# S1 T1 by quarters in the third and fourth pair of five more matrices of a relational graph layer

## The chip, the cores and the metric

The kernel runs on one core of one Trainium2 chip. The metric is device microseconds of one execution; the median over several runs is quoted, and the profile comes from one further execution.

## The reference

A graph layer over 1250 nodes with 1024 features, 20000 edges and 8 edge types:

```python
h = maximum(layernorm(x), 0)
u = h @ root + bias
for r in range(8):
    mask = edge_type == r
    sums = segment_sum(h[src] * mask[:, None], dst)       # by node
    cnt = segment_sum(mask, dst)
    u = u + (sums / maximum(cnt, 1)[:, None]) @ weight[r]
z = concatenate([u, h], axis=1) @ w_gate + b_gate
out = x + tanh(u) * z + h * (1 - z)
```

All in float32.

## The kernel before

**Matrices.** There are eleven products of the node features with a 1024 x 1024 matrix, in this order: eight `weight[r]` (s = 0 to 7), `root` (s = 8), the lower half of `w_gate` (s = 9), and the upper half (s = 10), which is applied to u. The text counts them one to eleven, so "matrix nine" is s = 8. The multiplication by `weight[r]` comes before the sum over edges: row blocks of h W_r go to `y` in DRAM, and rows of `y` are gathered edge by edge later.

**Pairs.** The 1250 nodes are ten blocks of 128 rows. Block i and block i + 5 form pair i; `product` handles one pair with one matrix, and `step(s, i)` calls it. Matrix s runs over pairs i = 0 to 4, the first to the fifth pair of the text. A pair is a 2 x 2 matrix of blocks (two blocks of rows by two halves of K), and `product` multiplies it with the 2 x 2 halves of the matrix in seven products instead of eight (Strassen's scheme in Winograd's form): A11 B11 (`p1`), A12 B21 (`p2`), S4 B22 (`p3`), A22 T4, S1 T1 (`p5`), S2 T2 and S3 T3 (`p7`), where S are sums of A blocks (`left`) and T of B blocks (`make_t1` to `make_t4`, L195 to L207). Each is four calls of a 128 x 128 by 128 x 512 matmul at L511.

**By quarters.** Two neighbouring pairs (first and second, third and fourth) together make some of the seven products once more in that scheme, on quarters: seven products, each two calls of 128 x 256 at L255, instead of eight calls of 128 x 512. Class `Second` does it for A12 B21 (`e` in `step`), `Third` for S4 B22 (`q`), `First` for A11 B11 (`first`), and `Fifth` for S1 T1 (`root`). Their own sums are made on VectorE in one shared buffer, `room`, four operations at a time: `sums` (L309 to L312) and `next_sums` (L315 to L318), the same two functions for `Third`, `First` and `Fifth`. So a class's `sums` can be made only when TensorE has read the ones before. `Fifth.begin`, `second`, `early` and `late` are the four places in the even pair's call where its matmuls stand; copies to and from its banks are L424, L432 and L439 on ScalarE, additions L434 and L445 on VectorE.

The function `fifths(s, i)` says in which matrices and pairs S1 T1 is made by quarters: in matrices two to five for all pairs, in six to ten for the first and second only.

**Banks.** PSUM has eight: `ps` four that rotate, `ps_b` two, `ps_n` and `ps_q` one each. `narrow[0]`, set from `fifths(s, i)`, sends the sums of S1 T1 and what is added to them into `sum_bank(0)`, which is `ps_n`, or `sum_bank(1)`, one of the four `ps` banks that is taken once and then held in `kept`. Where `narrow[0]` turns false, `kept` is cleared and the bank rotates again; the next time it is taken, `touch` (L134) writes it once with a matmul. The fourth pair's sum in `sum_bank(1)` is added to a row by L352 in `Third.last_to`; L351 and L353 beside it do so for `ps_n` and `ps_q`. In the fifth pair S1 T1 is made whole at L511, with `odd` 1.

**Order.** Each engine executes in the order in which the code issues. `product` calls `done()` at several places, the slots; each calls `between(j)`, which is `beside(j)` of `step` and, through it, the work of the edges: generators `edges` spread over the slots by `spread` (weights 10, 8, 13, 11, 8 for the five pairs). One step of it is `add_slot`: a gather of 128 rows of `y` by POOL (L1560) into one of five `got` buffers, and, some steps later, its addition to `u` on VectorE (L1565). It runs in matrices six to ten: one group of edges up to matrix eight, the second in nine and ten. `filled(name)` puts the matmuls by quarters of other classes between the seven products; the table of what goes where is `fill` in `step`. In a call with `Fifth` there is one slot more, `between(TICK)` in `p7`.

In the fourth pair's call, `fill["first"]` makes `e.seventh()` and, with `root`, `e.to_first(to)` (L282, L283), `q.first(...)`, `e.fourth()`, `e.to_second(t[0])` (L289, L290) and `e.fourth_to_second(t[0])` (L293): the matmuls that end A12 B21's quarters and the additions of them to the rows. `e.second()` later in that call takes a `ps` bank.

Of the kernel before, what the change touches and what calls it, by code (L numbers as in the profile page):

```python
# [21 lines left out]
def tile_rgcn_highway(  # L22
# [61 lines left out]
    TICK = 9  # L84
    LEFTS_AT = 6
    FIFTHS = (1, 4)
# [59 lines left out]
    def lead():  # L146

        return psum.tile([P, 512], F32, name="ps_b", bufs=2)
# [346 lines left out]
    def product(aop, w, to, between=lambda j: None, last=None, pieces=1, whole=True,  # L495
# [13 lines left out]
        def add(b, i, fresh=False, at=slice(0, Q), ks=range(KQ)):  # L509
            for k in ks:  # L510
                nc.tensor.matmul(b[:, at], aop[:, i, k, :], w.of[i][:, k, at],  # L511
                                 start=(fresh and k == 0), stop=(k == KQ - 1),
                                 skip_group_check=True)

        def done():
            between(step[0])
            step[0] += 1

        def filled(name):
            if fill and name in fill and fill[name]():  # L520
                done()
                return True
            return False
# [39 lines left out]
        def p1():  # L563
            if first is None:
                b = lead()
                add(b, A11, True)
            else:
                b = first.late() if head else first.to1
            if root and head:
                root.sums()  # L570
                first.fifth_to()
            nc.scalar.copy(c11, b)  # L572
            if root and head:
                root.second()
            done()
            filled("first")
            return b

        def p5(c=None):
# [14 lines left out]
        if root and head:  # L594
            root.begin()
            c = root.to0
            if inner:
                inner.c0 = c
            b = p1()
        elif first and head and early is None and "first" not in fill:  # L600
            c = inner.hold() if inner else sum_bank(odd) if narrow[0] else bank()
            add(c, S1, True, ks=range(KQ // 2))
            b = p1()
            p5(c)
        elif first and head:
            c = p5()
            b = p1()
        else:
            b = p1()
            if second:  # L610
                second()
                p2()
            c = p5()
# [74 lines left out]

    def fifths(s, i=0):

        return s >= FIFTHS[0] and (s <= FIFTHS[1] or i < 2)

    waiting, waiting_third, waiting_first, waiting_fifth = {}, {}, {}, {}
    at_call = [0, 0]
# [9 lines left out]
    def step(s, i, between=lambda j: None, second=None):  # L704

        two = paired(s, i)
        narrow[0] = fifths(s, i)
        if not narrow[0]:
            kept.clear()
# [6 lines left out]
        if two and i % 2 == 0:  # L716
            waiting[i] = Second(fac[s], i), t[0]
            if fifths(s, i):
                waiting_fifth[s, i] = Fifth(fac[s], i, room, p5_room)
# [13 lines left out]
        def beside(j):  # L733
# [28 lines left out]
            if (s, i, j) == (0, 0, 3) or (s > 0 and (i, j) == (3, int(thirds(s) or fifths(s)))):  # L762
                new.load_first()
# [205 lines left out]
    with ExitStack() as early:  # L969
# [20 lines left out]
        class Normed:  # L990
# [13 lines left out]
            def spread(self):  # L1004
                n = self.n
                nc.vector.bn_aggr(self.mv[:n], self.st[:n].rearrange("p a b -> p (a b)"))
                nc.scalar.activation(self.sd[:n], self.mv[:n, 1:2], AF.Sqrt, bias=eps[:n])
# [115 lines left out]
        first = ix1.tile([P, NCH], F32, name="first")  # L1123
# [391 lines left out]
        while going[0]:  # L1515
            s, i = next(steps)
# [11 lines left out]
    with ExitStack() as edges_part:  # L1528
# [89 lines left out]
        def spread(e, total, parts):  # L1618

            said = [0, 0]  # L1620
            parts *= 10

            def between(j):
                said[0] += (10, 8, 13, 11, 8)[at_call[0]]
                while said[1] < min(total, -(-total * said[0] // parts)):
                    next(e, None)
                    said[1] += 1
                if said[0] == parts:
                    for _ in e:
                        pass  # L1630

            return between
# [36 lines left out]
        def beside(e, total, s, i, last):  # L1669


            between = spread(e, total, 7 * ((last - s) * NP + NP - i))
            while s <= last:
                step(s, i, between)
                s, i = next(steps, (NM, 0))
            return s, i

        s, i = next(steps)
        while s <= EARLY:
            step(s, i)  # L1680
            s, i = next(steps)
# [21 lines left out]
        class Passes:  # L1703
# [45 lines left out]
            def next(self):  # L1749
                nc.vector.tensor_single_scalar(self.done, self.done, float(-MORE), op=OP.add)  # L1750
# [21 lines left out]
        while s < R0[1]:  # L1772
            step(s, i, on)
            s, i = next(steps)
# [14 lines left out]
        s, i = beside(first_group, sum(K[0]) + LATE + 1, s, i, R0[2] - 1)  # L1789
# [146 lines left out]
        while s < NM - 1:  # L1936
# [8 lines left out]
            s, i = next(steps, (NM, 0))  # L1945
# [86 lines left out]
```

## Time and profile before

| what | value |
|---|---|
| median of 3 runs | 1329.66 us (1327.80 to 1329.93) |
| profiled execution | 1325.06 us, its span 1323.3 us |
| granted TensorE clock | 0.998 |
| POOL L1560 gathers | 193, 1.32 us of POOL each |
| DVE L1565 edge additions | 193, 1.28 us each, 38.9 us idle before them |
| PE L511 into `ps_b` | 1464 matmuls, 658.3 us |

Busy times of the engines overlap each other, and those of pipelined matmuls overlap too, so costs of matmuls are taken from start to start. An engine's idle time matters only where another waits for it.

### The profile page before, as it was taken

How to read it: one execution, taken by the hardware profiler on the slowest of the kernel's cores; microseconds unless marked ns; L12 is line 12 of the kernel's file. 1: busy time of each engine (PE TensorE's matmuls, PEld its weight loads, DVE VectorE, ACT ScalarE, POOL GpSimd, SP SyncE). 2: the span in 40 equal slices, each digit the busy share in tenths (PEclk: the TensorE clock that was granted, in tenths of full speed). 3: DMA queues.
4: the chain of work that ended last, by engine and by line, in shares of the span. 5: the costliest groups of instructions: out<-in, count | busy, mean ns of one | idle time of the engine just before them, and what ended most of it. 6: DMA issues, size and time to landing. Idle time of an engine off the chain costs nothing.

```text
span 1323.3 us, 14353 instructions
## 1 busy us (share of the span) xinstructions
PE 1309.9 (99%) x4280; PEld 747.0 (56%) x4280; DVE 1032.2 (78%) x2171; ACT 277.9 (21%) x509; POOL 642.6 (49%) x981
## 2 busy tenths in 40 slices
PE   9999999999999999999999999999999999999997
PEld 5444565556455546655655655665565566544443
DVE  7768977797783776558977988897788889867974
ACT  3352121121112212211221211122122112122210
POOL 0001766666666675412453545456465546624732
PEclk9999999999999999999999999999999999999999
DMA  8976566753734253444748779788789957979961
GB/s 312 300 231 165 98 115 136 153 82 82 170 113 115 57 143 65 68 161 157 250 136 309 252 272 366 268 282 283 255 282 335 362 187 256 312 269 297 331 173 60
DMA packets 119397, 273.22 MB, mean 206 GB/s; under 512 B 33438, under 2 KB 45106, under 8 KB 119184
## 3 DMA queue, kind: packets, MB, share of 16 engines
q1 hardware_dynamic: 59120, 122.06, 31.7%
q0 software_dynamic: 44064, 118.20, 28.0%
q10 hardware_dynamic: 16128, 31.98, 7.9%
q8 instruction: 34, 0.56, 0.2%
q14 instruction: 51, 0.42, 0.1%
HBM read 210.73 MB, written 76.46 MB: 217 GB/s over the span
## 4 chain that ended last, share of the span: by engine, by line
PE 87%; DMA 4%; DVE 4%; issue 3%; POOL 1%; SPq 1%; ACT 1%; POOLq 0%; DVEq 0%
PE ps_b L511 42%; PE ps L255 19%; PE ps L511 10%; PE ps_n L511 4%; PE ps_b L255 4%; PE ps_n L255 3%; PE ps_q L255 2%; PE ps_q L511 2%; DMA xt<-in_x_dram 1%; DMA got<-hr_dram,node 1%; DMA w<-in_L_gnn_weight_dram 1%; DVE h_op L492 1%; DMA h_op<-in_L_gnn_b_gate_dram 0%; POOL out_dram L903 0%; SPq L983 0%
## 5 line engine op out<-in xcount | busy, mean ns | idle before, releaser
L511 PE MATMUL ps_b<-w,h_op 128*128 128x512 f32 x1464 | 658.3, 594 | 1.0 <-ACT row L615 0.8
L511 PEld LDWEIGHTS ps_b<-w,h_op 128*128 128x128 f32 x1464 | 275.2, 190 | 301.2 <-issue 292.7
L1560 POOL DMA_INDIRECT got<-y,idx x193 | 255.4, 1324 | 277.5 <-DVE u L1565 182.1
L1565 DVE SCALAR_TENSOR_TENSOR u<-got,w_of,u 128x1024 f32<-128x1024 f32 (+1 forms) x193 | 246.8, 1282 | 38.9 <-DMA got<-y,idx 36.3
L1209 POOL DMA_INDIRECT table<-row_col,at_i x157 | 183.3, 1168 | 119.4 <-issue 84.4
L511 PE MATMUL ps<-w,h_op 128*128 128x512 f32 (+1 forms) x392 | 174.1, 586 | 0.8 <-ACT row L589 0.8
L511 PEld LDWEIGHTS ps<-w,h_op 128*128 128x128 f32 x392 | 73.5, 190 | 84.0 <-issue 78.7
L255 PE MATMUL ps<-inner 128*128 128x256 f32 x420 | 106.1, 380 | 0.0
L255 PEld LDWEIGHTS ps<-inner 128*128 128x128 f32 x420 | 79.2, 190 | 20.7 <-issue 9.4
L255 PE MATMUL ps<-w,h_op 128*128 128x256 f32 x340 | 88.2, 382 | 1.0 <-ACT w L272 1.0
L255 PEld LDWEIGHTS ps<-w,h_op 128*128 128x128 f32 x340 | 63.7, 190 | 29.3 <-issue 20.7
L537 ACT COPY row<-ps_b 128x512 f32<-128x512 f32 x53 | 31.1, 586 | 225.4 <-PE ps_b L511 225.4
L615 ACT COPY row<-ps_b 128x512 f32<-128x512 f32 x54 | 31.7, 586 | 216.0 <-PE ps_b L511 216.0
L511 PE MATMUL ps_n<-w,h_op 128*128 128x512 f32 x168 | 75.6, 593 | 0.0
L255 PE MATMUL ps<-w,w 128*128 128x256 f32 x288 | 70.6, 380 | 0.0
L255 PEld LDWEIGHTS ps<-w,w 128*128 128x128 f32 x288 | 54.4, 190 | 17.2 <-issue 11.0
L1217 POOL MEMSET apart<- 128x1 f32 x471 | 54.6, 116 | 18.1
L659 ACT COPY row<-ps_b 128x512 f32<-128x512 f32 x40 | 23.4, 586 | 186.2 <-PE ps_b L511 165.1
L543 DVE TENSOR_TENSOR row<-row 128x512 f32<-128x512 f32 x44 | 30.2, 686 | 39.6 <-ACT row L537 39.6
L1326 DVE SCALAR_TENSOR_TENSOR junk<-k_bc,key_col,before 128x128 f32<-128x128 int16 x157 | 55.0, 350 | 4.2
L511 PEld LDWEIGHTS ps_n<-w,h_op 128*128 128x128 f32 x168 | 31.7, 190 | 37.7 <-issue 37.1
L572 ACT COPY row<-ps_b 128x512 f32<-128x512 f32 x54 | 31.8, 588 | 84.8 <-PE ps_b L511 80.5
(254 smaller groups left out, 1568.1 us busy)
## 6 DMA issues: line engine op xcount, KB each, us to landing
y<-row SPq DMA_DIRECT2D x72, 512.0 KB
w<-in_L_gnn_weight_dram ACTq DMA_DIRECT2D x21, 1024.0 KB
w<-in_L_gnn_weight_dram SPq DMA_DIRECT2D x10, 1024.0 KB
w<-lefts_dram SPq DMA_DIRECT2D x16, 512.0 KB
w<-in_L_gnn_w_gate_dram ACTq DMA_DIRECT2D x6, 1024.0 KB
k_bc<-keys_dram SPq DMA_DIRECT2D x39, 128.0 KB
l_bc<-los_dram SPq DMA_DIRECT2D x39, 128.0 KB
h_dram<-h_op SPq DMA_DIRECT2D x9, 512.0 KB
```

Of the source, the lines that this page charges most:

```text
L255: nc.tensor.matmul(p, a[:, k, :], b[:, k, :], start=(fresh and k == 0), stop=(k == 1), skip_group_check=True)
L511: nc.tensor.matmul(b[:, at], aop[:, i, k, :], w.of[i][:, k, at], start=(fresh and k == 0), stop=(k == KQ - 1), skip_group_check=True)
L537: nc.scalar.copy(d, b)
L543: nc.vector.tensor_add(c22, c if lone else c22, d)
L572: nc.scalar.copy(c11, b)
L615: nc.scalar.copy(c12, b)
L659: nc.scalar.copy(c21, b)
L1209: ins = nc.gpsimd.indirect_dma_start(out=table[:, :], out_offset=bass.IndirectOffsetOnAxis(ap=at_i[:n, c:c + 1], axis=0), in_=row_col[:n, ...
L1217: nc.gpsimd.memset(apart, 0.0)
L1326: nc.vector.scalar_tensor_tensor(junk, o["k_bc"][:, i, :], key_col[:, c:c + 1], before, op0=OP.is_equal, op1=OP.mult, accum_out=rank[:, c: ...
L1560: nc.gpsimd.indirect_dma_start(out=t[:n], out_offset=None, in_=y[g][:, :], in_offset=bass.IndirectOffsetOnAxis(ap=at[:n, d, k:k + 1], axis=0),
L1565: nc.vector.scalar_tensor_tensor(u[:n], t[:n], w, u[:n], op0=OP.mult, op1=OP.add)
```

## The change

`fifths` now holds for all matrices from the second on and all pairs, so S1 T1 of the third and fourth pair goes by quarters in matrices six to ten too. With it `narrow[0]` stays true in these matrices, and `kept` is not cleared in them. `fill` for the third pair is then the one for `root and q` (`e.first()` and `q.second` after S3 T3, `e.sixth()` at the end), and `e.seventh()` and `e.to_first(to)` move into the fourth pair's `fill["first"]`. In the odd pairs of matrices with both `Fifth` and `Third`, `filled("first")` now stands ahead of that slot's `done()`. `between` counts the slot `TICK` for the edges only in the first pair.

```diff
@@ product, p1
             if root and head:
                 root.second()
-            done()
-            filled("first")
+            if root and inner and not head:
+                filled("first")
+                done()
+            else:
+                done()
+                filled("first")
             return b
@@ 
     def fifths(s, i=0):
 
-        return s >= FIFTHS[0] and (s <= FIFTHS[1] or i < 2)
+        return s > 0
@@ spread
             def between(j):
-                said[0] += (10, 8, 13, 11, 8)[at_call[0]]
+                if j != TICK or at_call[0] == 0:
+                    said[0] += (10, 8, 13, 11, 8)[at_call[0]]
                 while said[1] < min(total, -(-total * said[0] // parts)):
                     next(e, None)
                     said[1] += 1
```

## The prediction

> **What bounds the kernel now.** I read the page's first and fourth parts, then windows over the stretches that the change touches, then the order of time on TensorE and VectorE around their ends. The page first (busy time by engine, and the shares of the chain that ended last):
>
> ```profile
> PE 1309.9 (99%) x4280; PEld 747.0 (56%) x4280; DVE 1032.2 (78%) x2171; ACT 277.9 (21%) x509; POOL 642.6 (49%) x981
> ...
> PE 87%; DMA 4%; DVE 4%; issue 3%; POOL 1%; SPq 1%; ACT 1%; POOLq 0%; DVEq 0%
> ```
>
> TensorE is the chain. Between 350 and 1170 us its matmuls stand end to end: the view of waits names one wait of PE there, of 0.5 us. So work taken from PE in matrices six to ten is time, unless PE begins to wait. The next view is windows over the third and fourth pair of one matrix: matrix five (which already makes S1 T1 of these pairs by quarters), then seven, nine and ten (which don't). Columns: length, busy time of PE, PEld, DVE, ACT, POOL, granted clock, DMA share, GB/s.
>
> ```profile
> 543.30:581.56 38.26, 38.26 (x139) 25.60 (x138) 20.36 (x52) 9.77 (x20) 14.13 (x15) 1.00 0.32 89
> ...
> 772.69:811.68 38.99, 38.99 (x125) 23.31 (x124) 31.18 (x37) 8.57 (x17) 23.52 (x21) 1.00 0.85 299
> ...
> 1002.99:1041.98 38.99, 38.99 (x126) 23.31 (x125) 30.93 (x38) 8.57 (x17) 26.25 (x21) 1.00 0.96 337
> 1118.15:1157.11 38.96, 38.96 (x126) 23.28 (x124) 31.31 (x41) 8.57 (x17) 24.83 (x19) 1.00 0.94 312
> ```
>
> Matrix five is the pattern for PE, but not for the rest: its DVE is busy 20.4 us of 38.3 and its DMA 0.32. In seven to ten DVE has 31 us of work in the same stretch, with the additions of gathered edges (L1565, 1.26 us each from start to start) in the same queue.
>
> **What PE saves.** Each f32 call of the code shows as two matmuls. S1 T1 of two pairs is now 16 matmuls of 512 columns, 3.435 us for each 8. By quarters it is seven products of 4 matmuls of 256 columns at 0.863 us. That is 6.87 against 6.04, a gain of 0.83. The pattern says the same with all that surrounds it: 38.26 less 0.11 for the two transposes of L1657 that only matrix five has is 38.15, against 38.99: 0.84 a matrix, 4.2 in five matrices. The bank that `sum_bank(1)` holds is no longer given up at the third pair, so the `touch` in matrices seven to ten goes: matrix six, which has none, takes 114.88 us from one fifth pair to the next (581.56 to 696.44) and matrix eight 115.13 (811.68 to 926.81). I take 0.25 each, 1.0 in four. Together 5.2 us off PE.
>
> The Trainium skill, "Perfetto Trace Analysis", section "Matmuls", holds larger matmuls to be more efficient where possible, which speaks against halving 512 columns; the rows above price the halves at no loss, so by the trace this part of the rule costs 0 here.
>
> **What it adds.** Per matrix DVE gets ten operations: `Fifth.sums` and `next_sums` (each 0.34 + 0.60 + 0.34 + 0.60 = 1.88, starts of the first pair's in matrix seven at 738.93 to 740.80), L434 and L445 (0.34 each): 4.4 us. ACT gets three copies (0.36, 0.37, 0.57: 1.3 us beside 8.6 of 39, free). DVE's idle in the stretch is 38.99 - 30.93 = 8.1 in matrix nine, 7.7 in ten, 7.8 in seven; afterwards some 2.6. POOL and SP keep their order; `TICK` not being counted in the third pair keeps the number of edge steps per call as it was, so DVE's additions only change places. On average DVE still fits, so I look for places where PE waits for one particular DVE instruction.
>
> **Waits that get shorter cover.** (a) `First.late` of the third pair followed 3.43 us of S1 T1; now only `root.begin`, 0.86. It needs `next_sums` (L316). In matrices six to nine that is done before the third pair starts, in ten 1.2 us after: 0.3 of stall there. (b) `root.early` needs `root.sums`, which stands behind one edge addition and has 4.3 us of PE work (`root.second` and S2 T2) as cover for 1.9: nothing. (c) `root.late` needs `next_sums` behind three or four edge additions; I count 1 to 2 us in hand, about 0.3 in ten. (d) `e.second` of the fourth pair needs L283, free bank; the second part of the change puts L282 to L293 ahead of that call's first slot, so one slot's additions (1.26 to 3.8 us) no longer stand before L293. Six or seven additions of the third pair still do; I count L283 within 1 us of the need in nine and ten. Moving it costs the edges nothing: they wait for DVE's turn either way. For (b) to (d) together I take 0.3, between 0 and 2.
>
> (e) The held bank. The fifth pair's S1 T1 goes, with `narrow[0]` now true, into `sum_bank(1)`: the very bank that the fourth pair's S4 sum lies in until L352 has added it to its row. Before, it went into a rotating bank and waited for nobody. L352 stands at the end of DVE's edge additions. DVE's and PE's order of time, first matrix nine, then ten (start, length, engine, line):
>
> ```profile
> 1045.77 1.29 DVE L1565 SCALAR_TENSOR_TENSOR u<-got,w_of,u 128x1024 f32<-128x1024 f32 x1 [2.67 <-DMA got<-y,idx]
> ...
> 1047.90 0.68 DVE L352 TENSOR_TENSOR row<-row,ps 128x512 f32<-128x512 f32 x1
> ```
>
> ```profile
> 1048.84 3.60 PE L511 MATMUL ps<-w,h_op 128*128 128x512 f32 x8
> ```
>
> ```profile
> 1165.06 0.68 DVE L352 TENSOR_TENSOR row<-row,ps 128x512 f32<-128x512 f32 x1
> ```
>
> ```profile
> 1163.98 3.60 PE L511 MATMUL ps<-w,h_op 128*128 128x512 f32 x8
> ```
>
> The PE rows are the fifth pair's S1 T1. L352 ends 0.3 us before it in nine and 1.8 us after it in ten. In six and seven it ends 5.2 before, in eight 3.6. Behind a waiting S1 T1 stands all of PE. With PE 0.84 earlier and DVE in place, the stall is 0.6 in nine and 2.6 in ten; that is the floor. The ceiling adds DVE's 4.4: 5.0 and 7.0, and 1.6 in eight (3.6 - 0.84 - 4.4).
>
> Between these: DVE's waits for gathers in the two stretches can swallow the new work (the view of DVE's waits, matrix nine from 1002.9 to 1049, then ten from 1117.9 to 1166; total, times, longest):
>
> ```profile
> DVE u L1565 <- DMA got<-y,idx: 8.6, 6, 2.7
> DVE row L543 <- ACT row L537: 1.8, 1, 1.8
> ```
>
> ```profile
> DVE u L1565 <- DMA got<-y,idx: 8.5, 5, 3.8
> ```
>
> In nine, both orders meet PE at L543 of the third pair, 16.5 us into the stretch (now about 16.1). Before, 8 of the 20 edge additions were done by then, now 6, and `Third.sums` too is still to come: 2 x 1.26 + 1.88 = 4.4 behind, 4.0 after the earlier L543. From there to L352 DVE waited 1.30 + 1.25 + 0.46 + 2.67 = 5.7 for gathers. But a gather is issued only when the addition five before it frees its buffer (POOL waited 182 us in all for that), and lands 6.1 us later in the median, 9 to 11 here; so a late DVE makes the next gathers late too. I let 1.5 of 4.0 be swallowed: L352 2.5 later, stall 3.1. In ten the 3.8 us wait in the middle comes before the last seven additions and takes up most of the lag; I put L352 1.0 later: stall 3.6. It includes (a) and (c), since PE only waits for what is left. Matrix eight: 0 to 1.6, taken as 0.
>
> **Sum.** 5.2 saved, 3.1 + 3.6 + 0.3 = 7.0 of stalls: +1.8 us. After matrix ten nothing changes: the last matrix is paced by PE, which waits 0.7 and 0.8 us there. The profiled execution took 1325.06 us (span 1323.3 and 1.8 around it), 4.6 below the median of 1329.66; so 1326.9 on its scale, 1331.4 on the runs'.
>
> The Trainium skill, "TensorE: Matmul & The Clock Gate", section "Why this matters for your kernels", wants no PE gap over about 3 us, or the clock falls to half; the longest wait of PE that the view of waits names is 1.4 us, so no row here shows it. By that rule two stalls of just over 3 us, each followed by some 3.4 us at half clock (its own figure), would add an estimated 3.4 in all. The sum above has none of it.
>
> **Rivals.** About 0.2% (2.7 us) is what a measurement of this kernel can tell from no change. One: the cover holds. DVE's idle of 8 us a stretch is larger than 4.4, the gathers land sooner because the additions come spread out instead of five in a row, and L352 comes early enough. For it: the second pair's call in these matrices, where DVE is busy 23.7 us of 24.1, shows no PE stall at all. Against it: matrix ten's L352 is already late. Stalls 0 to 2.5: 1324.5 to 1327, centre 1325.2. Two, the other side: the whole lag passes through to the held bank. For it: the gather loop above. Stalls 5.0 in nine, 7.0 in ten, 0 to 1.6 in eight, up to 2 in (b) to (d): 10 to 13 with part of it swallowed, 1334 to 1338, centre 1336. It is slower than 0.2% from a total stall of 7.9 on. Three: the change does less than it says. The order of the changed program shows the ten DVE operations and the 28 short matmuls in all five matrices, so 0.01.
>
> **Chances.** Forecast (stalls 4 to 9 us, 1328.5 to 1333.5) 0.54, of which 0.15 lies above 1332.4; rival one 0.21, almost all faster; rival two 0.20; the rest (another wait, a clock that falls) 0.05, of which 0.03 slower. Faster 0.20, same 0.42, slower 0.38. Range 1325.0 to 1336.5, which cuts the ends of both rivals.
>
> **What would show it.** Right: third and fourth pair at 38.15 us of PE in matrices six to eight; no L134 after the first third of the span; in nine and ten PE idle before the fifth pair's L511 into `ps`, ended by DVE L352, about 3 us each. Wrong: no such wait (rival one), more than 5 us of it (rival two), a wait for L316 or L283 of over 1 us, or a pair stretch that isn't shorter without a wait.

## The result, and the profile after

The changed kernel takes 1337.21 us (median; 1334.72 to 1337.86), the kernel before 1329.66: ratio 1.0054, interval 1.0040 to 1.0068. It is slower, by about 7 us. The forecast of 1331.4 was too low and the range, up to 1336.5, ends just below the result. The profiled execution took 1334.72 us (span 1332.9); in the experiments each ratio is to the kernel before on the same chip, whose median was 1325.5 in the first four, and 1328 to 1330 in the others.

The page after: busy time, then the chain that ended last by engine and by line.

```profile
PE 1308.3 (98%) x4336; PEld 757.2 (57%) x4336; DVE 1054.2 (79%) x2221; ACT 283.5 (21%) x524; POOL 652.0 (49%) x981
...
PE 76%; DVE 8%; DMA 7%; issue 6%; POOL 2%; SPq 1%; ACT 1%; POOLq 0%; DVEq 0%
PE ps_b L511 36%; PE ps L255 17%; PE ps L511 9%; DMA got<-y,idx 4%; PE ps_b L255 3%; PE ps_n L511 3%; PE ps_n L255 3%; DVE u L1569 2%; PE ps_q L511 2%; PE ps_q L255 2%; DMA xt<-in_x_dram 1%; DMA w<-in_L_gnn_weight_dram 1%; POOL got L1564 1%; DMA h_op<-in_L_gnn_b_gate_dram 0%; POOL out_dram L907 0%
```

PE's busy time fell a little, but its share of the chain fell from 87% to 76%. What came in is DVE, and the transfer of gathered rows: `DMA got<-y,idx` now has 4% of the chain. (Lines past 575 of the kernel are four further on: L1565 is now L1569, L1560 is L1564.)

Windows over the third and fourth pair after, matrix seven, then nine (length; busy PE, PEld, DVE, ACT, POOL; granted clock, DMA share, GB/s):

```profile
773.91:812.06 38.15, 38.15 (x138) 25.59 (x136) 31.55 (x43) 9.76 (x20) 18.11 (x16) 1.00 0.84 285
1003.94:1042.64 38.70, 38.32 (x137) 25.59 (x136) 30.49 (x43) 9.76 (x20) 20.63 (x18) 1.00 0.86 298
```

The saving is there to the hundredth: 38.15 us for 38.99. In nine the stretch holds a wait, and its DMA share, 0.96 before, is 0.86. The view of PE's waits, then the three fifth-pair S1 T1 in order of time, matrices eight, nine and ten:

```profile
PE ps L511 <- DVE row L352: 7.3, 3, 4.5
...
PE ps L255 <- DVE inner L316: 0.6, 1, 0.6
PE ps L255 <- DVE row L283: 0.4, 1, 0.4
```

```profile
934.82 3.70 PE L511 MATMUL ps<-w,h_op 128*128 128x512 f32 x8 [1.45 <-DVE row L352]
```

```profile
1054.21 6.04 PE L511 MATMUL ps<-w,h_op 128*128 128x512 f32 x8 [4.52 <-DVE row L352]
```

```profile
1173.27 1.98 PE L511 MATMUL ps<-w,h_op 128*128 128x512 f32 x4 [1.34 <-DVE row L352]
```

The wait is at the held bank, as forecast. In nine the matmuls behind it took 6.04 us for 3.60: the granted clock (the last column but two of the windows) had fallen.

```profile
1054.00:1058.00 4.00, 3.79 (x5) 1.71 (x6) 3.31 (x4) 0.00 (x0) 0.99 (x1) 0.50 1.01 372
1058.00:1062.00 4.00, 4.00 (x9) 1.79 (x9) 2.66 (x3) 0.00 (x0) 2.07 (x2) 0.88 1.03 419
1062.00:1066.00 4.00, 4.00 (x10) 1.71 (x9) 4.00 (x7) 0.58 (x1) 3.40 (x2) 1.00 1.02 410
```

**Account.** From the start of matrix five's fifth pair on PE (581.56 before, 583.87 after) to the transposes of u that follow matrix ten (1175.99, 1185.39) the changed kernel loses 9.40 - 2.31 = 7.1 us, about as much as the ratio says. Saved: 5.2. Lost, from start to start of matmuls: L352 1.6 + 4.7 + 1.5 = 7.8; L316, in eight and ten, 0.1 + 0.75; L283, in nine and ten, 0.55 + 0.2; the clock 2.4 (6.04 - 3.60). That gives +6.6; 0.5 is in smaller steps. The other 2.3 us, before matrix six, are left out of this account: about 1.5 of them are a wait for ScalarE in matrix five, where every engine still has the instructions of the kernel before in the same order (see "Not settled").

### The profile page after: what moved, and what is told of

Read it like the earlier page. It is cut to its first block, busy times and chain, and to the rows that moved or that the text cites. A ratio compares the mean times of both kernels' runs of the same rounds, so it can differ in the third digit from the quotient of the medians.

```text
span 1332.9 us, 14554 instructions
## 1 busy us (share of the span) xinstructions
PE 1308.3 (98%) x4336; PEld 757.2 (57%) x4336; DVE 1054.2 (79%) x2221; ACT 283.5 (21%) x524; POOL 652.0 (49%) x981
## 4 chain that ended last, share of the span: by engine, by line
PE 76%; DVE 8%; DMA 7%; issue 6%; POOL 2%; SPq 1%; ACT 1%; POOLq 0%; DVEq 0%
PE ps_b L511 36%; PE ps L255 17%; PE ps L511 9%; DMA got<-y,idx 4%; PE ps_b L255 3%; PE ps_n L511 3%; PE ps_n L255 3%; DVE u L1569 2%; PE ps_q L511 2%; PE ps_q L255 2%; DMA xt<-in_x_dram 1%; DMA w<-in_L_gnn_weight_dram 1%; POOL got L1564 1%; DMA h_op<-in_L_gnn_b_gate_dram 0%; POOL out_dram L907 0%
## 5 line engine op out<-in xcount | busy, mean ns | idle before, releaser
L1564 POOL DMA_INDIRECT got<-y,idx x193 | 258.2, 1338 | 283.3 <-DVE u L1569 183.9
L1569 DVE SCALAR_TENSOR_TENSOR u<-got,w_of,u 128x1024 f32<-128x1024 f32 (+1 forms) x193 | 247.1, 1282 | 29.5 <-DMA got<-y,idx 25.4
L511 PE MATMUL ps<-w,h_op 128*128 128x512 f32 (+1 forms) x352 | 158.9, 594 | 8.4 <-DVE row L352 7.3
L255 PE MATMUL ps<-inner 128*128 128x256 f32 x480 | 120.9, 380 | 0.6 <-DVE inner L316 0.6
L511 PEld LDWEIGHTS ps<-w,h_op 128*128 128x128 f32 x352 | 66.5, 193 | 87.0 <-issue 71.2
L255 PEld LDWEIGHTS ps<-inner 128*128 128x128 f32 x480 | 90.5, 190 | 26.1 <-issue 10.6
L255 PE MATMUL ps<-w,h_op 128*128 128x256 f32 x360 | 93.6, 382 | 2.6 <-issue 1.2
L255 PEld LDWEIGHTS ps<-w,h_op 128*128 128x128 f32 x360 | 67.3, 190 | 34.7 <-issue 24.0
L511 PE MATMUL ps_n<-w,h_op 128*128 128x512 f32 x128 | 57.6, 593 | 0.0
L543 DVE TENSOR_TENSOR row<-row 128x512 f32<-128x512 f32 x44 | 30.1, 684 | 21.8 <-ACT row L537 20.0
```

Source lines behind the costliest of these rows:

```text
L255: nc.tensor.matmul(p, a[:, k, :], b[:, k, :], start=(fresh and k == 0), stop=(k == 1), skip_group_check=True)
L543: nc.vector.tensor_add(c22, c if lone else c22, d)
L1564: nc.gpsimd.indirect_dma_start(out=t[:n], out_offset=None, in_=y[g][:, :], in_offset=bass.IndirectOffsetOnAxis(ap=at[:n, d, k:k + 1], axis=0),
L1569: nc.vector.scalar_tensor_tensor(u[:n], t[:n], w, u[:n], op0=OP.mult, op1=OP.add)
```

## The experiments

**First set: is it the held bank, and what precedes it?** The theory was that the whole loss is the wait for the held bank and the clock behind it. The rival: VectorE is late, and any place where PE needs it will show the wait.

The fifth pair's S1 T1 goes back into a rotating bank:

```diff
-        return s > 0
+        return s > 0 and (s <= FIFTHS[1] or i < NP - 1)
```

> The changed kernel, but the fifth pair of matrices six to ten is told that it is not narrow: S1 T1 of that pair goes into a rotating bank, as before the change, and the held bank is given up and touched again. Theory (the held bank costs the time: 7.8 us of waits for L352 in matrices eight to ten and some 2.7 us of a clock that falls after the longest of them): no wait for L352 at these places, no clock below 0.9 after them, the touches come back (1.0 us), so about 9.5 us less than the changed kernel: 1327 to 1328 us, 0.998 of the kernel before. The DVE delay must stay the same, so L352 still ends as late. Rival (DVE is simply short of time and any place will wait for it): the wait moves to the next bank of the rotation or to L353 and the time stays at 1334 or above.

Measured: 1.0011 (1.0002 to 1.0019). PE's waits from 560 to 1170 us:

```profile
PE ps L255 <- DVE inner L310: 2.5, 2, 1.3
PE ps L255 <- DVE inner L316: 2.5, 2, 1.9
PE ps L255 <- DVE row L283: 0.9, 2, 0.5
```

No L352, no fall of the clock, 0.43% won back. But the kernel is not faster than before: 5.9 us of waits for VectorE now stand elsewhere, the largest, 1.9 for L316 up to 1089.75, in the first pair of matrix ten. There VectorE has no idle time, while the DMA share (the last column but one) is low:

```profile
1084.00:1088.00 4.00, 3.88 (x11) 1.47 (x9) 4.00 (x3) 0.30 (x1) 3.70 (x2) 1.00 0.03 5
1088.00:1092.00 4.00, 2.25 (x10) 1.82 (x11) 3.96 (x9) 1.08 (x3) 2.91 (x3) 1.00 0.35 46
```

So in that pair it is VectorE's own work that keeps it late. Both sides were half right: the bank and the clock cost about 5.7 us more than the places to which the lateness moves.

The second part of the change alone, on the kernel before:

```diff
-            done()
-            filled("first")
+            if root and inner and not head:
+                filled("first")
+                done()
+            else:
+                done()
+                filled("first")
```

> The kernel before, with the second part of the change alone (in odd pairs with both classes the additions that end A12 B21 stand ahead of the slot; since the quarters of pairs three and four end at matrix five here, it acts in matrices two to five only). Theory: no difference, 1328 to 1331 us. Rival (the 1.6 us wait that the changed kernel shows in matrix five comes from this order): that wait is there, and the time is 1.5 us above the kernel before.

Measured: 1.0001 (0.9992 to 1.0009). It does nothing by itself. The traces differ from the kernel before's in the order of two operations of VectorE in matrix five, and nowhere else.

The quarters without it (the same lines put back in the changed kernel):

> The changed kernel without its second part: the quarters stay, but the slot's edge additions stand ahead of the additions that end A12 B21 again. Theory (the second part saves a wait for L283): PE waits longer at the second product of A12 B21 in matrices nine and ten, 1 to 3 us each instead of 0.4, and part of that comes back as a shorter wait for L352: 1337 to 1341 us. Rival (the second part matters little, since the wait for L352 behind it takes whatever is won): within 1 us of the changed kernel.

Measured: 1.0078 (1.0064 to 1.0091), so the second part is worth some 0.24% here, an estimate across two chips, as the intervals touch. PE's waits:

```profile
PE ps L255 <- DVE row L283: 6.8, 3, 2.6
PE ps L511 <- DVE row L352: 3.7, 2, 3.3
```

L283 is waited for in seven, nine and ten, by 2.6 us at most, and L352 for less in return: 10.5 us of both, for 7.7 in the changed kernel.

Fewer edge steps in the third and fourth call, more in the fifth:

```diff
-                    said[0] += (10, 8, 13, 11, 8)[at_call[0]]
+                    said[0] += (10, 8, 10, 10, 12)[at_call[0]]
```

> The changed kernel with the spread of the edge steps over the five calls 10, 8, 10, 10, 12 in place of 10, 8, 13, 11, 8: three or four edge additions fewer (1.28 us each) in the third and fourth call, as many more in the fifth. Theory (what delays L352 is the queue of additions ahead of it): L352 comes 3 to 5 us earlier, its waits are 0 to 1.5 us in nine and 0 in eight and ten, the clock stays at 1.0, and the time is 8 to 10 us below the changed kernel, 1327 to 1330 us. Rival (gathers set the pace and not DVE's turn): L352 as late as in the changed kernel, or new waits of 1 us or more in the fifth or the first call, and the time at 1333 or above.

Measured: 1.0067 (1.0054 to 1.0080). L352 did come earlier, with 0.9 us of wait in all, but PE waited 5.8 us for L316 and 1.1 for L310, mostly in the call of matrix ten's first pair, and the clock fell at 1092 us behind a wait of 2.1. The rival's times hold here, but not its reason (gathers that set the pace): from 1088 to 1092 us VectorE was busy throughout, at a DMA share of 0.05.

**Second set: what makes VectorE late?** My theory was its own queue: too many operations in one stretch. Half of each edge addition was left out to test it, the gathers staying whole:

```diff
-            nc.vector.scalar_tensor_tensor(u[:n], t[:n], w, u[:n], op0=OP.mult, op1=OP.add)
+            nc.vector.scalar_tensor_tensor(u[:n, :Q], t[:n, :Q], w, u[:n, :Q], op0=OP.mult, op1=OP.add)
```

> The changed kernel with each edge addition over half of its columns: 193 additions of 0.64 us or so in place of 1.28; the sums over edges of the other 512 columns are left out, the gathers stay whole. Theory (VectorE's queue, not the gathers' landing, makes L352 and the others late): no wait of TensorE for L352, L283, L310 or L316 of over 0.3 us, no fall of the clock, and the 5.2 us of saved TensorE work remain: 0.996 of the kernel before. Rival (the gathers' landing sets L352): it still ends late in matrix nine, 3 us or more of wait, and the time is 1.002 of the kernel before or above.

Measured: 1.0022 (1.0006 to 1.0038); the theory asked for 0.996. With some 10 us less of VectorE work in the stretch, L352 in matrix nine is as late as in the changed kernel, and what it is waited for is less only by the wait for L283 ahead of it. PE's waits in the same part of the span:

```profile
PE ps L511 <- DVE row L352: 3.9, 2, 2.7
PE ps L255 <- DVE row L283: 1.9, 1, 1.9
```

So VectorE's queue does not set L352 there, and the theory falls. In VectorE's order of time it stands idle 6.9 us for one gather. What is left to set L352 is the gathers' landing.

The slot after S3 T3 stands behind L353 in the fourth pair:

```diff
+        late = inner and not early and not head
@@ p7
-            done()
+            if not late:
+                done()
@@ then
                 inner.then(c)
+                if late:
+                    done()
                 done()
```

> The changed kernel, but in the fourth pair's call the slot after S3 T3 (two edge additions, 2.5 to 3.2 us of VectorE) stands behind L351 to L353 and not ahead of them. Theory (the held bank is waited for only because of what stands ahead of L352): matrix nine's wait 1.4 us in place of 4.7, those of eight and ten gone, no fall of the clock: 9 us less than the changed kernel if nothing else gets late; but VectorE's lateness itself stays, and in the run without the held bank it came back as 6.5 us of waits for L310 and L316 in matrices nine and ten, so I expect 1.001 of the kernel before. Rival (VectorE is late whatever the order, and the waits at L352 stay): 1.004 or above.

Measured: 1.0004 (0.9993 to 1.0016), no fall of the clock. L352 costs 0.4 us; L316, L283, L282 and L310 take 4.6 instead. As with the rotating bank, the lateness moves on, but at a smaller price.

The change in matrices six and seven alone:

```diff
-        return s > 0
+        return s > 0 and (s <= 6 or i < 2)
```

> The change in matrices six and seven alone; eight to ten as in the kernel before. Theory (there VectorE has time to spare: the changed kernel shows no wait in them): two times 0.84 us and one touch of 0.25 us are saved and no wait comes in: 1.9 us less than the kernel before, 0.9986 of it. Rival (VectorE's lateness is handed on to matrix eight and later): no gain, 1.000 or above, with waits of TensorE between 800 and 1170 us.

Measured: 0.9989 (0.9976 to 1.0002). The view of PE's waits names none from 565 to 1170 us. The expected 0.9986 lies in the interval, and so does no change.

An edge step at the slot `TICK` of the third pair, to fill VectorE's idle time at L445:

```diff
-                if j != TICK or at_call[0] == 0:
-                    said[0] += (10, 8, 13, 11, 8)[at_call[0]]
+                said[0] += (10 if j != TICK or at_call[0] == 0 else 0, 8, 11.375, 11, 8)[at_call[0]]
```

> The changed kernel, but the slot TICK counts for the edges in the third pair too, with the pair's weight 11.375 a slot in place of 13, so that the pair's additions are as many and one or two of them stand ahead of L445. Theory (VectorE idles 2.6 us at L445 in matrix nine, 1.4 us in eight and 1.3 us in ten, because it has nothing to add while TensorE runs up to it, and this idle time comes out again at L352): the idle time at L445 shrinks by 1.3 us or more, L352 ends 1 to 2.5 us earlier, and the time is 2 to 5 us below the changed kernel: 1.0015 to 1.004 of the kernel before. Rival (what is gained at L445 is lost to gathers that have not landed): L352 within 0.5 us of where it was, 1.0045 or above.

Measured: 1.0043 (1.0028 to 1.0058). The idle time at L445 in nine is gone, and L352 is waited for by 4.6 us all the same. So what is won at L445 is lost elsewhere, as the rival has it; the time lies between the two forecasts.

**Third set: the transfers.** The new theory: in the third and fourth pair of matrix nine L352 stands behind a fixed number of gathers, and comes when their bytes have been moved. The third pair's start up to the end of L352, in the kernel before, the changed one, and the one with half additions:

```profile
1003.00:1048.60 45.60, 45.60 (x141) 26.34 (x140) 34.85 (x42) 9.16 (x18) 28.47 (x23) 1.00 0.97 348
```

```profile
1003.90:1054.20 50.30, 45.41 (x153) 28.44 (x151) 39.15 (x53) 10.84 (x22) 26.58 (x23) 0.98 0.90 314
```

```profile
1003.20:1053.20 50.00, 45.45 (x153) 28.44 (x151) 28.71 (x51) 10.94 (x22) 25.29 (x23) 1.00 0.88 303
```

Length times GB/s is 15.9 MB before, 15.8 after and 15.2 with half additions: nearly the same load, at 0.97 of the DMA engines before and 0.90 and 0.88 after. VectorE's busy time, 39.2 or 28.7, makes no difference to the length. Half the additions and half the bytes of each gather:

```diff
-                out=t[:n], out_offset=None, in_=y[g][:, :],
+                out=t[:n, :Q], out_offset=None, in_=y[g][:, :].rearrange("r (h c) -> (r h) c", h=2),
```

> The kernel with halved edge additions, and the gathers halved too: 256 KB in place of 512 KB each, by the same 193 instructions (the other half of the sums over edges is left out). New theory (in matrices nine and ten the landing of the gathers sets L352: the additions that the change holds up keep the five buffers full, no gather is issued, the DMA engines go short of work, and the transfers come later): with half the bytes the gathers catch up; no wait for L352 over 0.5 us, L283 neither, and 0.996 to 0.998 of the kernel before, 5 us or more below the run with whole gathers and half additions. Rival (the additions' places in VectorE's queue, at any size, or the number of gathers, not their bytes): L352 waits of 2 us or more in nine again and the time at 1.001 or above.

Measured: 0.9955 (0.9942 to 0.9968), 0.67% below the run with whole gathers. The same stretch, and all that PE waits for between 560 and 1170 us:

```profile
1001.80:1047.60 45.80, 45.37 (x154) 28.47 (x152) 28.77 (x52) 10.77 (x22) 25.37 (x23) 1.00 0.72 240
```

```profile
PE ps L511 <- DVE row L352: 0.4, 1, 0.4
```

VectorE's work is that of the run with half additions; the bytes differ (11.0 MB), and L352 is back at 45.8. (The index counts half rows here, so other rows are fetched than the edges name; their number and size are as stated.) With half additions, then, the waits for L352 and L283 are the transfers'. Half the bytes with whole additions wasn't run.

The next matrix's first loads, one call earlier:

```diff
-            if (s, i, j) == (0, 0, 3) or (s > 0 and (i, j) == (3, int(thirds(s) or fifths(s)))):
+            if (s, i, j) == (0, 0, 3) or (s > 0 and (i, j) == (
+                    (2, 2) if s >= 7 else (3, int(thirds(s) or fifths(s))))):
                 new.load_first()
-            if (s, i, j) == (0, 0, 3) or (s > 0 and (i, j) == (3, 2)):
+            if (s, i, j) == (0, 0, 3) or (s > 0 and (i, j) == ((2, 3) if s >= 7 else (3, 2))):
                 new.load_next()
```

> The changed kernel, with the first two loads of the next matrix (1 MB each) issued in slots 2 and 3 of the third pair's call in place of slots 1 and 2 of the fourth's, in matrices eight to ten. Theory (transfers set L352, and the DMA engines go short at L434 and L445 of the third pair, at 0.56 and 0.67 busy over 8 us): the loads fill that place, the gathers of the fourth pair have the engines to themselves, L352 ends 2 to 4 us earlier in matrix nine, the clock does not fall, and the time is 3 to 7 us below the changed kernel: 1.000 to 1.003 of the kernel before. Rival (VectorE's queue): L352 as late as in the changed kernel; 1.0045 or above.

Measured: 1.0060 (1.0047 to 1.0073). The run is inconclusive. The loads go into the two buffers that hold the sums and copies of A12 B21's quarters in the current matrix (`spare`, used by `Second`), which the last pairs still read, so these pairs use the next matrix's values there and wait for the loads (2.3 us in eight and 1.5 in ten, 2.7 at the same place in nine, with a fall of the clock behind the two longer ones). L352 was not waited for at all, but the test is spoiled by the new waits.

The change in matrices six to eight, with the later slot:

```diff
-        return s > 0
+        return s > 0 and (s <= 7 or i < 2)
```

(and the edit of the slot after S3 T3 as above)

> The change in matrices six to eight alone (first group of edges), with the slot after S3 T3 of the fourth pair behind L353 in all matrices that have the class Third. Theory (matrices nine and ten cost more than they bring; eight brings its 0.84 us once L352 stands ahead of that slot): 3 times 0.84 us and two touches of 0.25 us, less 0.2 us of a wait for L310 in matrix nine: 2.8 us less, 0.998 of the kernel before. Rival (matrix eight's lateness passes on to nine, whose gathers have no room): 1.000 or above, with over 2 us of waits for VectorE between 920 and 1060 us.

Measured: 0.9983 (0.9975 to 0.9992). It is faster than both kernels, by what was worked out (0.998); the view of PE's waits names none between 560 and 1170 us. The later slot was not run by itself on the kernel before; that kernel has no wait of PE there which it could take away.

The change in matrix nine alone:

```diff
-        return s > 0
+        return s > 0 and (s <= FIFTHS[1] or i < 2 or s == 8)
```

> The change in matrix nine alone; six to eight and ten as in the kernel before. Theory (the lateness is made inside matrix nine's own third and fourth pair: buffers held up at L309 to L445, gathers issued late): L352 is waited for by 3 to 4.7 us, the clock falls for some 4 us after it, and less 1.1 us of savings the time is 4 to 6.5 us above the kernel before: 1.003 to 1.005 of it. Rival (it is carried over from matrices six to eight): a wait under 1.5 us, no fall of the clock, and 0.9995 to 1.0005.

Measured: 1.0062 (1.0045 to 1.0080), as much as the whole change or more.

```profile
PE ps L511 <- DVE row L352: 4.7, 1, 4.7
PE ps L255 <- DVE row L283: 0.8, 1, 0.8
```

The lateness is made inside matrix nine. Its stretch has 0.93 of DMA share, and L352 ends 50.8 us after its start.

## Why the prediction was wrong, point by point

**The saving** was right: 0.84 a matrix, and the touches 0.25 (between the marks of matrices six and seven the changed kernel gains 0.84 and 1.09). 5.2 us in all.

**The place** was right: (e), the bank that the fourth pair's S4 sum lies in, read by L352. (b) shows no wait, and (a), (c) and (d) are L316 and L283, 1.6 us where 0.6 was forecast.

**The step that failed** is "I let 1.5 of 4.0 be swallowed: L352 2.5 later, stall 3.1." L352 came 4.7 us later (45.6 to 50.3 from the third pair's start), and the wait was 4.7: close to the ceiling of 5.0 and to rival two. The lag itself was read rightly: at L543 of the third pair six additions were done, and `Third.sums` was still to come. What failed is the swallowing. From there to L352 VectorE waited 5.7 us for gathers before, and after 5.3 and 0.7 more for which the view names nobody: nothing of the 4.0 was taken up. Only ahead of L543 did waits for gathers go (2.9 before, none after), and there the new operations have waits of their own for PE. VectorE's waits in matrix nine after, from 1003.9 to 1054.2:

```profile
DVE u L1569 <- DMA got<-y,idx: 5.3, 4, 2.7
DVE ps L445 <- PE ps L255: 2.6, 1, 2.6
DVE inner L309 <- PE ps L255: 1.6, 1, 1.6
DVE u L1569 <- issue: 0.7, 1, 0.7
```

While it stands there for PE it frees no buffer. POOL's order of time shows the issue of gathers held up, with longer idle times in front of a gather (in brackets) than any of the kernel before there, the longest of which was 2.96:

```profile
1010.21 1.79 POOL L1564 DMA_INDIRECT got<-y,idx  x1 [4.66 <-DVE u L1569]
...
1024.26 1.79 POOL L1564 DMA_INDIRECT got<-y,idx  x1 [4.81 <-DVE u L1569]
```

Time that the DMA engines lose there (a share of 0.56 to 0.67 in three of the five 4-us windows from 1010 to 1030) was not made good: from 1030 to 1054 their share is 0.99 or more in each 4 us. The prediction shows the row that warns of it (matrix nine, DMA share 0.96) and reads only VectorE's column in it. "On average DVE still fits" asked about VectorE alone, beside DMA engines at 0.96: with 10 us less of VectorE work L352 was as late; with half the bytes as well it was in time. Whether the transfers alone set it in the changed kernel isn't shown. Of the 50.3 us VectorE is busy for 39.2; without its waits for gathers L352 would end 44 to 45 us in, an estimate from these rows, against 45.6 in the kernel before.

**The balance.** Between the forecast +1.8 and the 7.1 of the account lie 5.3 us: 2.4 of the clock, which the sum put at nothing; 1.7 of matrix eight, also put at nothing; 1.6 of L352 in nine; 0.25 of L283 there beyond the 0.3 for (b) to (d); 0.5 of smaller steps; less 1.15 in ten.

**Matrices eight and ten.** Eight was taken at 0 and came at its ceiling, 1.6. Ten was forecast at 3.6 with what L316 takes in it, and measured 1.5 + 0.75 + 0.2: behind 7 us of lost time in nine, the transfers may have had time to catch up, which no run shows. All waits together were 9.4 us where the sum had 7.0.

**The clock** was left out of the sum, since no row of before showed one; it cost 2.4 us. The Trainium skill, "TensorE: Matmul & The Clock Gate", section "Why this matters for your kernels", was weighed beside the sum with an estimated 3.4 us for two gaps over 3 us, so 1.7 for one. One gap was that long, 4.5 us, and the clock behind it cost 2.4.

**Rivals.** The second (the whole lag passes through) was the nearest: 1334 to 1338, its stall in nine 5.0, its gather loop the cause. It had 0.20. Its 7.0 in ten did not come, and the clock made up for that, so that its time came so near is in part luck.

**Not settled.** That full buffers are what starves the DMA engines is read from the order of time; more than five buffers wasn't tried. That a fixed load sets L352 is not borne out by two runs: with an edge step at `TICK` 17.5 MB were moved in the stretch (0.98 of the DMA engines), with nine alone 16.8 (0.93), and L352 was as late. Of the 1.7 MB more at `TICK`, the view of DMA queues puts 0.7 in the queue of the gathers, of which 21 were issued in place of 20, and 0.9 in the largest of the other queues; loads and stores issued in the stretch are the same in number.

The wait for ScalarE in matrix five, 1.2 us and more, shows in the profiles of the changed kernel, and of the runs from half additions on, but in none of the first four, which ran on another chip. Up to 564 us, before the first reordered operation and behind the start of each of these waits, PE, VectorE, ScalarE and GpSimd go through the same instructions in the same order in these profiles as in that of the kernel before, so a changed order is not the cause; what is, wasn't looked into.

## What to carry to other kernels

Before filling an engine's idle time, ask what it is idle for. Here it waited for transfers whose engines were at 0.97; operations put ahead of the additions that free a buffer held up the gathers behind them, and the delay arrived whole at the next bank that someone held. Price a new operation by its own waits as well as its length, and make such a change matrix by matrix, where the columns for DMA and VectorE both leave room: three of the five matrices, with one slot moved, gave 0.17% (0.08 to 0.25); all five lost 0.54%.

## What the runs showed of the hardware

After every wait of PE of 3.3 us or more the granted clock was 0.50 for 4.6 to 5.8 us (matrix nine of the changed kernel, of the quarters without the new order, of the edge step at `TICK`, and of nine alone). It fell 2.3 to 3.3 us into the wait and stayed down for 6.8 us in all. Below that it went either way: it fell, for 3.4 us, behind waits of 2.1 (weights), 2.3 and 2.7 (loads earlier) and 2.7 (matrix five with the edge step at `TICK`), and stayed at 1.00 behind one of 2.6 (quarters without the new order, 805 us) and one of 2.7 (half additions, 1053 us). So a length of 3 us is no sharp border in these runs.
